# The W2 product of a fused four-layer graph kernel: one level of Strassen against two

## The chip, the cores and the metric

The kernel runs on one core of one Trainium2 chip, in fp32. The metric is the device time in microseconds of one execution. The profile gives a span, from the first to the last instruction.

## The reference

The input x is 128 graphs of 128 nodes with 256 features; adj is one 128 x 128 matrix for all graphs. Four layers follow each other, each adding its result to x:

```python
h = relu(layernorm(x)); x = x + gated_message_passing(h, adj)           # layer 0
h = relu(layernorm(x)); x = x + causal_attention(h, adj, Wqkv, Wo)      # layer 1
h = relu(layernorm(x)); x = x + gcn(h, adj * adj, W1, W2, W3)           # layer 2
h = relu(layernorm(x)); x = x + gcn_batchnorm(h, adj, bW1, bW2, ...)    # layer 3
# gcn:  h = relu(A @ (h @ W1));  h = relu(A @ (h @ W2));  return A @ (h @ W3)
```

W1 is 256 x 512, W2 is 512 x 1024, W3 is 1024 x 256. The change concerns `h @ W2`, which for each node is the largest product of the whole chain. A batch normalisation in layer 3 needs the mean and variance over all nodes, so layer 3 ends only when all graphs have passed.

## The kernel before, in words

The 128 graphs go in 32 groups of four (`G = 4`, `NG = 32`), T = 512 nodes a group. In the first pass every group runs through layers 0 to 2 and the first half of layer 3 in SBUF; its x goes to DRAM as `X3` (POOL's queue), its layer-3 values as `Z` (SP's queue). The second pass reads `Z` and `X3` again and finishes layer 3.

*Strassen.* Most weight products use the Winograd form of Strassen's algorithm at one level: seven products of quarter matrices for eight. `seven_of` makes the weights' sums once, `sums` makes the sums of an activation on DVE (four element-wise operations), and `seven` runs the products in the order 0, 1, 4, 5, 2, 6, 3 on three PSUM banks px, py, pz: products 0, 5, 6 and 3 accumulate in px, 4 and 2 in pz. Between them partial results leave the bank: `kept` copies px or pz to SBUF on ACT, and `put` adds such a copy to a bank on DVE (three of the four outputs) or copies it on ACT (the fourth). So a product that accumulates on px has to wait for the engine that reads px before it.

*The W2 product.* `layer1` ends with u = relu(.. @ W1) and uT = (A u) transposed: 32 matmuls `pmu`, four evictions of 128 x 512 by DVE in `mixed`, and `sums` over uT. `layer2` then computes h2T = relu(W2^T uT) in two halves, `wide(0)` and `wide(1)`, each a `seven` with products of four matmuls (two 128-row blocks of the output, two 128-deep pieces, 256 columns moving: `columns_by_half`, L404). `put` adds on DVE (L678) and ACT applies ReLU (L679); after the last product come the four sums of that half (L370 to L373). Then the product with W3 (`rows_by_half`, L387: 128 columns moving), `pr` with a2T, the addition to x and the store to `X3`. W2 and its sums lie in SBUF for the whole pass.

*The order.* The layers are generators; each `yield` ends a step. One turn of the group loop runs layer 2 of group g, layer 1 of g+1, layer 0 of g+2 and layer 3 of g-1, and the string `TURN` says which generator does its next step: A layer 0, B layer 1, C layer 2, D layer 3, b and d the first steps of the next ones. The last group has the string `FINAL`, and `FILL` starts the first groups. What the string gives is the program order on all engines; the framework then orders each engine's instructions by when they are ready, with program order as priority, and places the waits. PSUM is eight banks, all of one pool.

```python
    TURN = "CCCBCCABBDABBCABBDDCBADCDDBDCCDBACBCCABCCACbBCBBCBCBBCBCBCdB"
    ...
    for g in range(NG):
        if g + AHEAD < NG:
            load_x(g + AHEAD)
        ...
        for k in TURN if g < LAST else FINAL:
            next(stream[k], None)
```

Of the kernel before, what the change touches and what calls it, by code (L numbers as in the profile page):

```python
# [8 lines left out]
FP = mybir.dt.float32  # L9
AF = mybir.ActivationFunctionType  # L10
ALU = mybir.AluOpType
# [11 lines left out]
def kernel(  # L23
# [60 lines left out]
    def rows(w):  # L84
        return w.rearrange("(c p) f -> p c f", p=P)
# [29 lines left out]
    w1 = weights.tile([P, DC, H1], FP, name="w1")  # L115
    w2 = weights.tile([P, HC1, H2], FP, name="w2")
    w3 = weights.tile([P, HC2, D], FP, name="w3")
# [54 lines left out]
    dinv = small.tile([P, 1], FP, name="dinv", bufs=1)  # L172

    nc.sync.dma_start(wqkv, rows(Wqkv))
    nc.sync.dma_start(wo, rows(Wo))
# [62 lines left out]
    for dst, src in ((ain, adj_sb), (aout, adjT)):  # L238
        nc.vector.tensor_scalar(pos, src, 0.0, None, ALU.is_gt)
        nc.vector.scalar_tensor_tensor(f, src, 0.0, pos, ALU.min, ALU.add)  # L240
        nc.vector.tensor_tensor(dst, f, adj_sb, ALU.mult)

    SETS = {}
    plain = {"qv": 0, "u": 0}

    def prepare():
# [22 lines left out]
        yield  # L269
        SETS["2"] = seven_of(w2, "w2")  # L270
        yield
# [92 lines left out]
    def sums(engine, a, extra, s3=None):  # L364


        a11, a12, a21, a22 = a
        s3 = a21 if s3 is None else s3
        s1, s2, s4 = (extra[:, i] for i in range(3))
        engine.tensor_tensor(s1, a21, a22, ALU.add)  # L370
        engine.tensor_tensor(s2, s1, a11, ALU.subtract)
        engine.tensor_tensor(s4, a12, s2, ALU.subtract)
        engine.tensor_tensor(s3, a11, a21, ALU.subtract)  # L373
        return a11, a12, s4, a22, s1, s2, s3

    def quarters_t(aT):

        return quarters(aT)
# [33 lines left out]
    def seven(product, put, shape, name, pool=None):  # L412

        def kept(pb, i):
            t = (pool or w).tile(shape, FP, tag="kept", name=f"{name}_t{i}", bufs=6)
            nc.scalar.copy(t, pb)  # L419
            return t  # L420

        px = bank(shape, f"{name}_x")
        product(0, px, True)
        t1 = kept(px, 1)
        yield
        py = bank(shape, f"{name}_y")
        product(1, py, True)
        put((0, 0), py, t1)
        yield
        pz = bank(shape, f"{name}_z")  # L430
        product(4, pz, True)
        t5 = kept(pz, 5)
        yield
        product(5, px, False)
        t2 = kept(px, 2)
        yield
        product(2, pz, False)
        put((0, 1), pz, t2)
        yield
        product(6, px, False)  # L440
        put((1, 1), px, t5)
        yield
        product(3, px, False)
        put((1, 0), px, None)
        yield

    def layer0(g, bs=ALL):
# [42 lines left out]
        mine = slice(bs[0], bs[-1] + 1)  # L490
        nc.vector.tensor_copy(cmbT[:, mine, :], pc)
        yield
# [13 lines left out]
    def layer1(g, bs=ALL):  # L506
# [93 lines left out]
        pT = tile_of(g, bs, [P, G, P], "pT", f"pT_{g}", 1)[:, bs[0] : bs[-1] + 1, :]  # L600
        nc.vector.tensor_copy(pT, pp)
        yield
# [35 lines left out]
        else:  # L638
# [9 lines left out]
            yield  # L648
        uT = tile_of(g, bs, [P, HC1, T], "uT", f"uT_{g}", 1)
        mixed(uT, u, a2T, f"pmu_{tail}", (nc.vector.tensor_copy,), bs)  # L650
        if bs[-1] == G - 1:
            ex = w.tile([P, 3, HC1 // 2, T // 2], FP, tag="us", name=f"us_{g}", bufs=1)
            US[g] = sums(nc.vector, quarters_t(uT), ex)
        yield

    def layer2(g):

        xt, us = X[g], US[g]
        h2T = w.tile([P, HC2, T], FP, tag="h2T", name=f"h2T_{g}", bufs=1)

        a11, a12, a21, a22 = quarters_t(h2T)
        ex = w.tile([P, 3, HC2 // 2, T // 2], FP, tag="h2s", name=f"h2s_{g}", bufs=1)
        h2s = (a11, a12, ex[:, 2], a22, ex[:, 0], ex[:, 1], a21)

        def wide(q):
            def put(ij, pb, other):
                i, j = ij
                j = j * HC2 // 2 + 2 * q
                dst = h2T[:, j : j + 2, i * T // 2 : (i + 1) * T // 2]
                if other is None:  # L670
                    nc.scalar.activation(dst, pb, AF.Relu)
                    mine = slice(2 * q, 2 * q + 2)
                    sums(
                        nc.vector,
                        [a[:, mine] for a in (a11, a12, a21, a22)], ex[:, :, mine],
                    )
                else:
                    nc.vector.tensor_tensor(dst, pb, other, ALU.add)  # L678
                    nc.scalar.activation(dst, dst, AF.Relu)  # L679

            return seven(
                columns_by_half(us, SETS["2"], 2 * q), put, [P, 2, T // 2], f"p2_{g}_{q}"
            )

# [11 lines left out]

        yield from wide(0)
        late = wide(1)
        for _ in range(6):
            yield next(late)  # L700
# [13 lines left out]
    def layer3(g):  # L714
# [3 lines left out]
        gT = w.tile([P, DC, T], FP, tag="dT", name=f"gT_{g}", bufs=2)  # L718
        mixed(gT, h, ahT, f"pg_{g}", (nc.vector.tensor_copy,))
        ex = w.tile([P, 3, 1, T // 2], FP, tag="ex", name=f"gs_{g}", bufs=2)  # L720
# [30 lines left out]

    TURN = "CCCBCCABBDABBCABBDDCBADCDDBDCCDBACBCCABCCACbBCBBCBCBBCBCBCdB"

# [5 lines left out]
    def part(f, g):  # L759
        return f(g) if 0 <= g < NG else iter(())  # L760
# [14 lines left out]
    assert all(next(stream[k], k) == k for k in "acbdA")  # L775
    bs, ds = part(layer1, 1), stream["p"]
    next(bs)
    for g in range(NG):
# [217 lines left out]
```

## Time and profile before

| | |
|---|---|
| time before, median of 2 runs | 2605.85 us (2605.66 to 2606.03) |
| the profiled execution | 2605.08 us, span 2603.0 us |
| one turn in the middle of the first pass | 70.80 us |
| first pass, prologue included | to about 2322 us |
| second pass and output | to 2603 us |

The profile names an instruction by its line in the kernel, its engine and operation, and the tiles it writes and reads; "128x512 f32" is partitions by elements. PE is the matmul engine and PEld its weight loads, which overlap; DVE, ACT and POOL are the vector, scalar and general engines; SPq is the queue of SyncE, from which most transfers are issued. Each fp32 matmul of the source is two records. "Idle before <- releaser" says how long an engine stood and which instruction ended the wait.

### The profile page before, as it was taken

To read this page: it belongs to the slowest core of one execution; us is meant where nothing else is said; L and a number is where in the kernel's file an instruction comes from. 1 tells how busy PE (TensorE), PEld (TensorE's weight loads), DVE (VectorE), ACT (ScalarE), POOL (GpSimd) and SP (SyncE) were. 2 spreads that over 40 slices of the span, in tenths; PEclk is the share of its full clock that TensorE was granted. 3 is DMA by queue.
4 is the path that set the end of the run, shared out by engine and by line. 5 is a ranking of instruction groups with operands and counts; after the bars stand their busy time and mean duration, and the time that the engine had idled before them with its cause. 6 is when DMAs were issued, how large, how long until landed. Compare 5 with 4: busy or idle time off the path is not lost.

```text
span 2603.0 us, 40680 instructions
## 1 busy us (share of the span) xinstructions
PE 2538.9 (98%) x15281; PEld 2283.6 (88%) x15281; DVE 1914.1 (74%) x4820; ACT 1283.8 (49%) x2575; POOL 291.3 (11%) x581
## 2 busy tenths in 40 slices
PE   5999999999999999999999999999999999999996
PEld 4899999999999999999999999999999999888875
DVE  7777777777777777777777777777777776567776
ACT  4544454444445444454444444554445444346656
POOL 2110111111110111111111110111011111000001
PEclk8999999999999999999999999999999999999998
DMA  3000000000100000000000000010000000035449
GB/s 133 15 33 33 33 28 22 33 33 34 33 25 25 33 33 33 33 33 21 29 33 33 33 25 25 33 33 33 33 33 25 25 25 25 25 136 181 175 172 395
DMA packets 49560, 143.06 MB, mean 55 GB/s; under 512 B 4162, under 2 KB 23124, under 8 KB 45396
## 3 DMA queue, kind: packets, MB, share of 16 engines
q1 hardware_dynamic: 42164, 116.48, 12.3%
q0 software_dynamic: 6480, 23.60, 2.5%
q8 instruction: 120, 1.97, 0.3%
q14 instruction: 76, 0.62, 0.1%
q10 hardware_dynamic: 720, 0.39, 0.1%
HBM read 73.48 MB, written 66.98 MB: 54 GB/s over the span
## 4 chain that ended last, share of the span: by engine, by line
PE 91%; ACT 3%; DVE 2%; DMA 2%; issue 1%; POOL 1%; DVEq 0%; SPq 0%; ACTq 0%; POOLq 0%
PE p_x L404 17%; PE p_x L387 9%; PE p_z L404 8%; PE pmu L359 4%; PE p_z L387 4%; PE pz_x L404 4%; PE p_y L404 4%; PE pu_x L387 4%; PE po_x L879 3%; PE pg L359 2%; PE ps L577 2%; PE pm L359 2%; PE pm L497 2%; PE p_y L387 2%; PE pqv_x L534 2%; PE pr L707 2%
## 5 line engine op out<-in xcount | busy, mean ns | idle before, releaser
L345 ACT ACTIVATE h<-x,sh,rs 128x256 f32<-128x256 f32 x512 | 268.9, 590 | 370.5 <-POOL sh L342 370.5
L404 PE MATMUL p_x<-uT,w 128*128 128x256 f32 x1024 | 242.2, 379 | 0.0
L679 ACT ACTIVATE h2T<-h2T 128x512 f32<-128x512 f32 x192 | 120.5, 628 | 229.0 <-DVE h2T L678 228.5
L404 PEld LDWEIGHTS p_x<-uT,w 128*128 128x128 f32 x1024 | 189.7, 190 | 23.2
L334 DVE BATCH_NORM_STATS2 st<-x 128x6 f32<-128x256 f32 x512 | 191.4, 416 | 3.9 <-DMA x<-in_x_dram 1.8
L338 POOL TENSOR_SCALAR rs<-mv 128x4 f32<-128x4 f32 (+1 forms) x131 | 31.1, 237 | 1393.8 <-ACT h2T L679 1026.9
L456 DVE SCALAR_TENSOR_TENSOR gs<-h,gw 128x256 f32<-128x256 f32 x384 | 161.9, 422 | 33.4 <-ACT h L345 27.5
L419 ACT COPY p_t<-p_x 128x512 f32<-128x512 f32 (+1 forms) x192 | 96.8, 504 | 108.4 <-PE p_x L404 101.6
L339 POOL TENSOR_TENSOR rs<-rs,nhalf 128x4 f32<-128x4 f32 (+1 forms) x131 | 149.5, 1141 | 0.0
L359 PEld LDWEIGHTS pmu<-a2T,u 128*128 128x128 f32 x1024 | 119.4, 192 | 15.3 <-issue 15.1
L387 PEld LDWEIGHTS p_x<-w,h2T 128*128 128x128 f32 x1024 | 124.3, 192 | 3.3
L387 PE MATMUL p_x<-w,h2T 128*128 128x128 f32 x1024 | 124.6, 275 | 0.0
L632 ACT ACTIVATE u<-u 128x512 f32<-128x512 f32 x93 | 58.7, 631 | 133.7 <-DVE u L631 133.7
L868 ACT ACTIVATE zi<-zi,sh_bn,sc_bn 128x512 f32<-128x512 f32 x124 | 97.3, 812 | 49.1 <-DMA zi<-z 19.8
L404 PE MATMUL p_x<-us,w_s 128*128 128x256 f32 x512 | 121.3, 379 | 0.0
L404 PE MATMUL p_z<-us,w 128*128 128x256 f32 x512 | 121.2, 379 | 0.0
L404 PE MATMUL p_x<-uT,w_s 128*128 128x256 f32 x512 | 121.1, 379 | 0.0
L404 PE MATMUL p_y<-uT,w 128*128 128x256 f32 x512 | 121.0, 379 | 0.0
L404 PE MATMUL p_z<-us,w_s 128*128 128x256 f32 x512 | 120.9, 379 | 0.0
L359 PE MATMUL pmu<-a2T,u 128*128 128x128 f32 x1024 | 119.5, 275 | 0.0
L708 DVE TENSOR_TENSOR x<-pr,x 128x512 f32<-128x512 f32 x64 | 43.7, 683 | 90.4 <-PE pr L707 90.4
L404 PEld LDWEIGHTS p_z<-us,w 128*128 128x128 f32 x512 | 97.2, 190 | 13.6 <-ACT p_t L419 0.4
(300 smaller groups left out, 6183.8 us busy)
## 6 DMA issues: line engine op xcount, KB each, us to landing
z<-zo SPq DMA_DIRECT2D x62, 512.0 KB, 2.6
zi<-z SPq DMA_DIRECT2D x31, 1024.0 KB, 4.8
x<-x POOLq DMA_DIRECT2D x32, 512.0 KB, 3.4
x<-in_x_dram SPq DMA_DIRECT2D x31, 512.0 KB, 4.0
out_dram<-x3i SPq DMA_DIRECT2D x30, 512.0 KB, 12.3
x3i<-x SPq DMA_DIRECT2D x19, 512.0 KB, 5.1
x3i<-x POOLq DMA_DIRECT2D x13, 512.0 KB, 11.5
w<-in_L_gnn_W_dram SPq DMA_DIRECT2D x1, 2048.0 KB
```

The costliest lines, as they stand in the source:

```text
L334: nc.vector.bn_stats(st[:, k, :], xt[:, b, :])
L339: nc.gpsimd.tensor_tensor(rs, rs, nhalf[:, :n], ALU.pow)
L345: nc.scalar.activation(h[:, b, :], xt[:, b, :], AF.Relu, bias=sh[:, k : k + 1], scale=rs[:, k : k + 1])
L359: nc.tensor.matmul(pm[:, k, :], src[:, b, c * P : (c + 1) * P], aT, start=True, stop=True)
L387: nc.tensor.matmul(pb[:, rr, :], a_r[r][:, c, rr * P : (rr + 1) * P], b_r[r][:, c, :wide], start=(first and rr == 0 and c == 0), stop=(c = ...
L404: nc.tensor.matmul(pb[:, jj, :], b_r[r][:, c, at : at + P], a_r[r][:, c, :], start=(first and jj == 0 and c == 0), stop=(c == nk - 1), ski ...
L419: nc.scalar.copy(t, pb)
L456: nc.vector.scalar_tensor_tensor(gs, h[:, b, :], 1.0, gw[:, i, :], ALU.mult, ALU.mult, accum_out=gl[:, k, i : i + 1],)
L632: nc.scalar.activation(dst, dst, AF.Relu)
L679: nc.scalar.activation(dst, dst, AF.Relu)
L868: nc.scalar.activation(z, z, AF.Relu, bias=sh1[:, j : j + 1], scale=sc1[:, j : j + 1],)
L879: nc.tensor.matmul(pb, BW2R[r][:, c, :], a_r[r][:, c, :], start=(first and c == 0), stop=(c == FC // 2 - 1), skip_group_check=True,)
```

## The change

W2's product goes from one level of Strassen to two: each of the seven products of quarters is itself done by seven products of sixteenths, 49 in all, each of two matmuls with 128 columns moving and no accumulation over depth. In detail:

- `prepare_w2` replaces `seven_of(w2)`: it makes the seven weights of the first level and, of each, the seven of the second, on DVE, and stores them in DRAM as `W2R`. W2 no longer has its own place in SBUF; during preparation it lies in the buffer that later holds uT.
- `load_w2` reads one of the seven sets (128 x 7 x 256 floats) for each part of each group, on SP's queue, into three rotating buffers.
- The end of `layer1` writes uT in a new layout with room for all second-level sums; its evictions alternate between DVE and ACT; the sums are eleven operations.
- `layer2` runs seven parts in the order 0, 1, 4, 5, 2, 6, 3. Each is one `seven` with 128 x 256 results that go to one of seven homes; additions on whole quarters (128 x 1024) then form h2T's quarters, ReLU on ACT works on whole quarters, and `sums` runs once over the whole h2T.
- Copies that move from DVE to ACT: `cmbT` in layer 0, `pT` in layer 1, one of two gT evictions in layer 3. `kept` has five buffers for six.
- `TURN` is another string with the same steps.

```diff
-    w2 = weights.tile([P, HC1, H2], FP, name="w2")
...
+    def load_w2(r, n):
+        SETS["2", r] = weights.tile([P, 7, H2 // 4], FP, tag="w2r", name=f"w2_{n}_{r}", bufs=3)
+        nc.sync.dma_start(SETS["2", r], W2R[r])
+
+    def prepare_w2():
+        b11, b21, b12, b22 = quarters(w2)
+        t1, t2, t4n = w2t
+        nc.vector.tensor_tensor(t1, b12, b11, ALU.subtract)
+        nc.vector.tensor_tensor(t2, b22, t1, ALU.subtract)
+        nc.vector.tensor_tensor(t4n, b21, t2, ALU.subtract)
+        nc.vector.tensor_tensor(b12, b22, b12, ALU.subtract)
+        stage = None
+        for n, r in enumerate(SEVEN):
+            b = (b11, b21, b22, t4n, t1, t2, b12)[r]
...
+            nc.vector.tensor_tensor(ex[:, 0], c12, c11, ALU.subtract)
+            nc.vector.tensor_tensor(ex[:, 1], c22, ex[:, 0], ALU.subtract)
+            nc.vector.tensor_tensor(ex[:, 2], c21, ex[:, 1], ALU.subtract)
+            nc.vector.tensor_tensor(c12, c22, c12, ALU.subtract)
+            nc.sync.dma_start(
+                W2R[r][:, :4, :].rearrange("p (c h) f -> p c h f", c=2),
+                b.rearrange("p c (h f) -> p c h f", h=2),
+            )
+            nc.sync.dma_start(W2R[r][:, 4:, :], ex)
+
+    SEVEN = 0, 1, 4, 5, 2, 6, 3
...
-        SETS["2"] = seven_of(w2, "w2")
+        prepare_w2()
...
-            t = (pool or w).tile(shape, FP, tag="kept", name=f"{name}_t{i}", bufs=6)
+            t = (pool or w).tile(shape, FP, tag="kept", name=f"{name}_t{i}", bufs=5)
...
-        nc.vector.tensor_copy(cmbT[:, mine, :], pc)
+        nc.scalar.copy(cmbT[:, mine, :], pc)
...
-        nc.vector.tensor_copy(pT, pp)
+        nc.scalar.copy(pT, pp)
...
-        uT = tile_of(g, bs, [P, HC1, T], "uT", f"uT_{g}", 1)
-        mixed(uT, u, a2T, f"pmu_{tail}", (nc.vector.tensor_copy,), bs)
...
+            evict = nc.scalar.copy if c % 2 else nc.vector.tensor_copy
+            evict(dst, pm.rearrange("p (i b) n -> p i (b n)", b=2))
...
+            three(0, 2)
+            s1, s2, s4, s3 = v[:, 4], v[:, 5], v[:, 2], v[:, 6]
+            nc.vector.tensor_tensor(s1, v[:, 6], v[:, 3], ALU.add)
+            nc.vector.tensor_tensor(s2, s1, v[:, 0], ALU.subtract)
+            nc.vector.tensor_tensor(s4, v[:, 1], s2, ALU.subtract)
+            nc.vector.tensor_tensor(s3, v[:, 0], v[:, 6], ALU.subtract)
+            three(2, 7)
+            fourth(0, 7)
...
+            def product(s, pb, first):
+                for jj in range(2):
+                    nc.tensor.matmul(
+                        pb[:, jj, :], b_s[s][:, jj * P : (jj + 1) * P], a_s[s],
+                        start=(first and jj == 0), stop=True, skip_group_check=True,
+                    )
...
+        def wide():
+            x_, t1, t2 = (ex[:, i] for i in range(3))
+            homes = {0: x_, 1: a11, 4: a22, 5: t1, 2: a12, 6: t2, 3: a21}
+            then = {
+                0: (), 1: ((a11, x_),), 4: (), 5: ((x_, t1),), 2: ((a12, a22), (a12, x_)),
+                6: ((x_, t2), (a22, x_)), 3: ((a21, x_),),
+            }
+            for n, r in enumerate(SEVEN):
+                if n < 6:
+                    load_w2(SEVEN[n + 1], g)
+                elif g < LAST:
+                    load_w2(SEVEN[0], g + 1)
+                of_r = one_of_seven(r, homes[r])
+                for _ in range(3):
+                    next(of_r)
+                yield
+                for _ in of_r:
+                    pass
+                for dst, src in then[r]:
+                    add(dst, src)
+                if then[r] and r != 5:
+                    relu(then[r][-1][0])
+                yield
+            sums(nc.vector, (a11, a12, a21, a22), ex)
...
-        mixed(gT, h, ahT, f"pg_{g}", (nc.vector.tensor_copy,))
+        mixed(gT, h, ahT, f"pg_{g}", (nc.scalar.copy, nc.vector.tensor_copy))
...
-    TURN = "CCCBCCABBDABBCABBDDCBADCDDBDCCDBACBCCABCCACbBCBBCBCBBCBCBCdB"
+    TURN = "CBCACDCABCBBBDDBBACCCABCDBDCDACBDBBCCACCBCBBBABDbBCCBCCBCCBd"
```

`three(lo, hi)` makes three of the four second-level sums for the parts lo to hi - 1 at once; `fourth(0, 7)` makes the last one for all seven parts, in place. In the text, w0a and w0b are the two steps of the part r = 0: the products 0, 1, 4, and then 5, 2, 6, 3.

## The prediction

> **What bounds the kernel now.** I read the page's busy times and slices first, then the windows of one turn, then the timelines of PE and DVE inside that turn, and last the waits of the DMA queue. The page:
>
> ```profile
> PE 2538.9 (98%) x15281; PEld 2283.6 (88%) x15281; DVE 1914.1 (74%) x4820; ACT 1283.8 (49%) x2575; POOL 291.3 (11%) x581
> ...
> PE   5999999999999999999999999999999999999996
> ...
> DVE  7777777777777777777777777777777776567776
> ```
>
> PE is full from the second slice on; DVE runs at seven tenths. In the windows of one turn (us; then busy us and instructions of PE, PEld, DVE, ACT, POOL; granted clock; DMA share; GB/s), whole, and cut where the second half of the W2 product has its sums:
>
> ```profile
> 1062.40:1133.20 70.80, 70.80 (x440) 64.53 (x439) 52.84 (x138) 34.33 (x70) 8.66 (x18) 1.00 0.08 31
> 1062.40:1113.00 50.60, 50.60 (x297) 46.11 (x296) 43.56 (x115) 26.63 (x56) 6.84 (x14) 1.00 0.10 37
> 1113.00:1133.20 20.20, 20.20 (x145) 18.42 (x144) 9.28 (x24) 7.69 (x15) 1.81 (x4) 1.00 0.04 15
> ```
>
> A turn is 70.8 us with no idle PE time at all. DVE has 18.0 us to spare, but unevenly: 7.0 us in the first 50.6 us (86% busy) and 10.9 us in the tail. The PE timeline gives the two matmul rates:
>
> ```profile
> 1062.41 1.89 PE L404 MATMUL p_x<-uT,w 128*128 128x256 f32 x8
> 1064.14 1.89 PE L404 MATMUL p_y<-uT,w 128*128 128x256 f32 x8
> ...
> 1109.35 1.95 PE L387 MATMUL p_y<-w,h2T 128*128 128x128 f32 x16
> 1111.13 1.95 PE L359 MATMUL pm<-a2T,h 128*128 128x128 f32 x16
> ```
>
> Each matmul of the source is two records. Start to start, four of 256 columns take 1.73 us (0.4325 each), eight of 128 columns 1.78 us (0.223 each): half the columns cost 52%, weight loads included. For DVE, start to start:
>
> ```profile
> 21.94 1.21 DVE L214 TENSOR_TENSOR w_s<-w 128x1024 f32<-128x1024 f32 x1
> 23.07 0.61 DVE L476 SCALAR_TENSOR_TENSOR m<-aout,gt,m 128x128 f32<-128x128 f32 x2
> ...
> 1079.13 0.42 DVE L373 TENSOR_TENSOR gT<-gT 128x256 f32<-128x256 f32 x1
> 1079.46 0.43 DVE L372 TENSOR_TENSOR gs<-gT,gs 128x256 f32<-128x256 f32 x1
> ...
> 1111.51 0.68 DVE L373 TENSOR_TENSOR h2T<-h2T 128x512 f32<-128x512 f32 x1
> 1112.11 0.68 DVE L372 TENSOR_TENSOR h2s<-h2T,h2s 128x512 f32<-128x512 f32 x1
> ```
>
> So packed DVE work costs 0.335 us for 256 elements, 0.60 for 512, 1.13 for 1024; between these I interpolate (640: 0.73; 896: 1.0).
>
> **What the Trainium skill says.** "VectorE: DVE Perf Modes", the perf-mode tier table: fp32 tensor_tensor has only the single rate, and with any PSUM operand too. The trace agrees: 0.69 us for 512 elements in L372 (SBUF) and in L678 (PSUM), so every added sum is paid by the element. "Perfetto Trace Analysis", Matmuls: independent groups should rotate through PSUM banks so that an eviction overlaps the next group, and larger matmuls are more efficient. The trace agrees on both: 0.223 is more than half of 0.4325, and no product waits for its eviction here, because each is followed by 0.9 to 1.8 us of other products.
>
> **The change, part by part.**
>
> *PE.* Removed per group: 14 products of four 256-column matmuls, 14 x 1.73 = 24.2 us. Added: 98 of 128 columns, 98 x 0.223 = 21.9 us. Gain 2.3 us a turn, all on the path; a turn of pure PE would be 68.5 us.
>
> *DVE, removed per turn:* 6 additions and 8 sums of layer2 at 512, 4 sums of uT, 2 of 4 uT evictions, and the copies cmbT, pT and one gT that go to ACT: 23 x 0.60 = 13.8 us. *Added:* sums of uT: three of 256, four of 512, three of 640, one of 896 (1.0 + 2.4 + 2.2 + 1.0 = 6.6 us); 21 PSUM additions of 256 (7.0); seven additions of 1024 that join the quarters (7.9); four sums of 1024 (4.5). Together 26.0, net +12.2. DVE has 52.8 + 12.2 = 65.0 us of work in a 68.5 us turn, 95%: its spare time falls from 18.0 to 3.5 us. This is the heart of the case.
>
> *ACT.* Five more copies of 512 (0.5 us packed), 28 copies of 256 (0.3) for 6 copies and 2 ReLUs of 512, four ReLUs of 1024 for six of 512: about 14.7 added, 7.2 removed. 34.3 becomes 42 us, 61%: no bound, but it now stands between products that follow each other closely.
>
> *The new waits.* (1) One product is now 0.45 us of PE, and inside the second half of each of the 49-product's seven parts the order is 5, 2, 6, 3: product 3 writes the bank that DVE must have read after product 6, with nothing between in the source. A 256-element DVE read is 0.42 us, behind whatever DVE has in hand. Other PE work must be moved in. That the order does this is seen in the first turn of before, where a product is split so that pp and pc get in as they become ready:
>
> ```profile
> 105.26 0.59 PE L404 MATMUL p_x<-us,w_s 128*128 128x256 f32 x2
> 105.69 0.38 PE L599 MATMUL pp<-ident,p 128*128 128x128 f32 x2
> ```
>
> There is no idle PE time around it, so I count most of these waits as filled. (2) The last uT eviction is followed by 6.6 us of sums, and the very last (`fourth`) makes the operand of product 6 of the first part. It is ready about 0.75 + 6.6 = 7.4 us after the last pmu matmul; PE reaches product 6 after w0a (1.34), hT (0.87) and two products (0.9), 3.1 us. That is a hole of 4.3 us each turn; before, the whole uT sums were 2.4 us and first needed after two products of 1.73. The second part's products, gT and its like can fill it. Bounds: 0 if all is filled, 4.3 if nothing is; I take 2.2. (3) DVE starts each turn 6.6 us behind, and by the running sum of the steps in the new turn (from its start to the end of the part r=6: PE 37.2 us, DVE 37.0) it catches up only in the tail. PE then meets DVE at nearly every part; for DVE and ACT arriving late I take 0.8 us a turn, bounds 0 and 4. The cover that hid such waits, DVE's 18 us, is gone. Total stall taken: 3.0 us, turn 68.5 + 3.0 = 71.5.
>
> *DMA.* Seven loads of 128 x 7168 B (0.92 MB) a turn. The page has 4.0 us from issue to landing for 512 KB and 4.8 for 1 MB, so about 4.7; three buffers let a load start when the product three before it is done, some 6 us of its own PE work ahead. 6.4 MB over 71 us adds 90 GB/s to 31; the second pass moves 170 to 180 at under half DMA share. Free, if the loads are not held in SP's queue:
>
> ```profile
> SPq L108 <- DMA x<-x: 1062.0, 28, 60.9
> ```
>
> The load of x stands in SP about 38 us a turn waiting for the X3 store of the group before; W2 loads queued behind it would come late. SP's issues are ordered by readiness (in the prologue the load for group 3 is at 25.6 us, ahead of BW2T's store at 81.8, which the source has first), and the three buffers are filled by then, so I take 0; the other end is 5 us a turn.
>
> *Ends.* prepare_w2 is 4 x 1.13 + 28 x 0.335 = 13.9 us of DVE against 4.5, in a prologue where PE is busy 116 of 145 us: +6 taken (0 to 10). The last turn has no other group's work to fill: its PE gain is lost again in the 4.5 us of late sums before the third product and in hole (2), which gives +4 (0 to 10).
>
> **Sum.** Against the profiled execution (2605.08, span 2603.0, so 2.1 us lie around it): 31 turns x (71.5 - 70.8) = +22, ends +10: 2637; the median shown is 0.8 higher: 2638 us. A difference under 2% (52 us) can't be told from no change in this kernel.
>
> **The rivals.**
> - *Clean fill* (chance 0.12): stall under 1 us, say 0.5. For it: PE shows not one gap in a steady turn of before. Against: 95% DVE. 31 x (69.0 - 70.8) + 8 = -48: 2558, and 2541 with no stall.
> - *DVE becomes the bound* (0.36): slower. In a turn of before DVE is idle in a dozen places for data (3.5 for p_z, 2.8 for pr, 1.7 for ACT's mT). If 9 of the 18 us of such idling cannot be packed, the turn is 65.0 + 9 = 74 us: 31 x 3.2 + 10 = +109: 2715. It decides from 70.8 - 65.0 = 5.8 us of DVE idle time a turn; every us above costs 31. For it: the pmu evictions, pr and the two sums that follow each other leave the tail thin in DVE work (8 us of idling there by the running sum) while the front has none to spare. Against: the new turn puts the parts 5 us apart.
> - *W2 loads late* (0.07): 5 us of PE waiting a turn on DMA and part of the gain kept: 31 x 3.5 + 10: 2725.
> - *No gain on PE*: 128-column matmuls bound by weight loads. The L387 rate already contains them (16 loads in 1.78 us); 0.02, about 2700 with the stalls.
> - *Forecast, gain eaten* (0.43): stall 1.5 to 4.5 us, 2591 to 2685, likeliest 2638.
>
> **How the numbers follow.** Clean fill gives 0.07 of "faster" and 0.05 of "same"; the forecast 0.38 "same", 0.05 "slower"; DVE bound 0.32 "slower", 0.04 "same"; the rest is slower. Faster 0.07, same 0.47, slower 0.46. The range leaves out the best of the clean fills and the worst of the DVE-bound cases: 2560 to 2750.
>
> **What would show it.** Right: PE busy near 96% of a steady turn of 71 to 72 us, DVE at 63 to 66 us of it, PE's waits naming DVE sums of uT at product 6 and DVE additions at product 3, no wait on w2. Wrong: DVE work far from 65 us, PE waits on the W2 loads, a turn under 70, or PE idle on ACT copies, which I hold hidden.

## The result, and the profile after

The changed kernel takes 2834.41 us (median of two runs, 2832.83 to 2835.99) against 2605.85: 1.0877 times as long (95% interval 1.083 to 1.0924), slower by 229 us. The forecast was 2638, the range 2560 to 2750; the time lies outside it. The profiled execution took 2835.99 us with a span of 2834.2.

The page of after, busy times:

```profile
PE 2624.6 (93%) x17969; PEld 2374.0 (84%) x17969; DVE 2279.3 (80%) x5484; ACT 1510.8 (53%) x3315; POOL 355.3 (13%) x581
```

PE is no longer full: 98% became 93%, and at a lower granted clock (0.968 over the execution, 0.992 before), so a part of its "busy" time is slow time. DVE went from 74% to 80%. Two turns of after, in the windows (us; then busy us and instructions of PE, PEld, DVE, ACT, POOL; granted clock; DMA share; GB/s):

```profile
1009.64:1088.39 78.75, 74.42 (x523) 68.11 (x522) 63.87 (x158) 41.43 (x93) 10.90 (x17) 0.96 0.32 109
1323.95:1399.47 75.52, 71.36 (x524) 65.60 (x523) 63.85 (x158) 41.43 (x93) 10.23 (x17) 1.00 0.34 114
```

Same work, but 78.75 us at clock 0.96 and 75.52 us at clock 1.00. Before, every steady turn was 70.79 or 70.80 us; now the 29 turns between the first and the last range from 75.5 to 80.1 us, 77.87 on average. That is the first thing to see: one part of the loss is always there, another comes and goes.

The part that is always there is a hole, a stretch in which PE stands, that begins 6.8 us into a turn. The turn that starts at 1009.64, from the timeline:

```profile
1013.21 0.61 PE L748 MATMUL p_x<-uT,w 128*128 128x128 f32 x4
...
1014.18 0.41 DVE L407 TENSOR_TENSOR uT<-uT 128x256 f32<-128x256 f32 x1
...
1015.09 2.63 POOL L379 TENSOR_TENSOR sh<-sh,rs 128x4 f32<-128x4 f32 x1
...
1016.07 0.39 PE L748 MATMUL p_x<-uT,w 128*128 128x128 f32 x2
...
1016.98 0.69 DVE L722 TENSOR_TENSOR uT<-uT 128x512 f32<-128x512 f32 x1
1017.76 2.07 ACT L382 ACTIVATE h<-x,sh,rs 128x256 f32<-128x256 f32 x4 [3.76 <-POOL sh L379]
1019.74 0.35 ACT L457 COPY p_t<-p_x 128x256 f32<-128x256 f32 x1
...
1020.14 1.22 PE L748 MATMUL p_x<-uT,w 128*128 128x128 f32 x4 [3.69 <-ACT p_t L457]
1021.16 1.06 PE L748 MATMUL p_z<-uT,w 128*128 128x128 f32 x4
```

Read it backwards from the 3.69 us in which PE stood. Product 5 of the part r = 0 adds to px, so it waits until ACT has copied product 0 out of px (L457). That copy takes 0.35 us and px was complete by 1013.8, but on ACT it stands behind `h` of layer 3's norm (L382, four activations, 2.07 us), and `h` waits for GpSimd's `sh` (L379), the multiplication of two 128 x 4 tiles. That operation took 2.63 us here; it ends with the run of VectorE's uT sums that began ahead of it. The wait of 3.69 us comes in each of the 29 turns between the first and the last, and is the largest of PE's (us in total, times, longest):

```profile
PE p_x L748 <- ACT p_t L457: 109.4, 31, 3.7
```

The same chain in before, in the turn that starts at 1058.84 (L342 is the shift, L345 `h`, L419 the copy, and the product at 1068.47 is product 5):

```profile
1062.98 0.20 POOL L342 TENSOR_TENSOR sh<-sh,rs 128x4 f32<-128x4 f32 x1
1063.22 2.08 ACT L345 ACTIVATE h<-x,sh,rs 128x256 f32<-128x256 f32 x4 [5.29 <-POOL sh L342]
...
1065.20 0.56 ACT L419 COPY p_t<-p_x 128x512 f32<-128x512 f32 x1
...
1068.47 1.89 PE L404 MATMUL p_x<-us,w_s 128*128 128x256 f32 x8
```

The copy stood behind `h` in before too. But there the norm's step was ahead of the sums in the string, the shift took 0.20 us, and the copy was done 6.9 us into the turn (1065.76), while PE came to product 5 after 9.6 us: 2.7 us to spare. In after the copy is done 10.45 us into the turn (1020.09), 3.5 later, of which the drawn-out shift is 2.4, and PE would come to product 5 after 6.65 us (1016.29), 3.0 earlier, because the products ahead of it are short. 2.7 - 3.5 - 3.0 is a lateness of 3.8 us. The new order and the short products make about half of it each.

The part that comes and goes is the clock. In the turn at 1009.64, the records of a product behind the hole (p_z above) take 1.06 us, and one product follows the other after 0.85 us. The turn at 1323.95 has the same hole, and its products behind it are at full rate, 0.61 us and every 0.45:

```profile
1334.44 0.71 PE L748 MATMUL p_x<-uT,w 128*128 128x128 f32 x4 [3.69 <-ACT p_t L457]
...
1336.11 0.61 PE L748 MATMUL p_z<-uT,w 128*128 128x128 f32 x4
```

The granted clock was one half for 6.82 us of the first turn, from within the hole on:

```profile
1018.70:1025.52 6.82, 5.38 (x25) 5.38 (x26) 5.40 (x10) 3.26 (x9) 0.00 (x0) 0.50 0.23 79
```

The Trainium skill, "TensorE: Matmul & The Clock Gate", Part 1, says that an idle window of about 3.4 us halves TensorE's clock until it has been busy for about as long again, and that the window runs freely, so that the moment varies. The trace agrees that it varies, and on the length: with the same 3.69 us of waiting, 12 of the 29 turns have a stretch of 3.41 us at half rate, 12 have one of 6.83, and five have none. Those five take 76.06 us on average (one 75.52, four 76.2), so the half rate is worth 77.87 - 76.06 = 1.8 us a turn. The trace does not agree on 3.4 us of idling as a lower limit: PE had stood for 2.0 to 3.1 us in the 3.41 us before each of the 24 stretches, and in runs below, waits of 2.97, 2.84 and 2.09 us were followed by half rate in some turns.

W2's loads answered the forecast, from the page's DMA issues (KB each, us to landing):

```profile
w<-W2R SPq DMA_DIRECT2D x224, 896.0 KB, 4.7
```

No product of a steady turn waits for one. The last turn has the only long one, 2.93 us.

Where the 231.2 us between the two spans went: from the first pmu matmul of the first turn to that of the last group are 31 turns, 2401.8 us after and 2187.8 before, +214.0; the prologue is +8.2 (81.3 against 73.1 us), what follows the last turn +9.0.

### The profile page after: what moved, and what is told of

It reads as the page before. It is cut to its first block, busy times and chain, and to the rows that moved or that the text cites. A ratio compares the mean times of both kernels' runs of the same rounds, so it can differ in the third digit from the quotient of the medians.

```text
span 2834.2 us, 48744 instructions
## 1 busy us (share of the span) xinstructions
PE 2624.6 (93%) x17969; PEld 2374.0 (84%) x17969; DVE 2279.3 (80%) x5484; ACT 1510.8 (53%) x3315; POOL 355.3 (13%) x581
## 5 line engine op out<-in xcount | busy, mean ns | idle before, releaser
L748 PE MATMUL p_x<-uT,w 128*128 128x128 f32 x3584 | 557.4, 282 | 116.2 <-ACT p_t L457 109.4
L748 PEld LDWEIGHTS p_x<-uT,w 128*128 128x128 f32 x3584 | 495.5, 194 | 146.7 <-ACT p_t L457 121.7
L382 ACT ACTIVATE h<-x,sh,rs 128x256 f32<-128x256 f32 x512 | 266.2, 589 | 300.6 <-POOL sh L379 300.6
L457 ACT COPY p_t<-p_x 128x256 f32<-128x256 f32 x512 | 189.8, 371 | 276.6 <-PE p_x L748 160.5
L748 PE MATMUL p_z<-uT,w 128*128 128x128 f32 x1792 | 303.4, 292 | 13.3 <-DVE uT L407 11.3
L748 PEld LDWEIGHTS p_z<-uT,w 128*128 128x128 f32 x1792 | 260.7, 204 | 28.4 <-DVE uT L407 17.2
L764 DVE TENSOR_TENSOR h2T<-h2T,h2s 128x1024 f32<-128x1024 f32 x128 | 155.7, 1216 | 48.0 <-ACT h2T L757 48.0
L767 ACT ACTIVATE h2T<-h2T 128x1024 f32<-128x1024 f32 x128 | 135.4, 1058 | 62.6 <-DVE h2T L764 62.5
L457 ACT COPY p_t<-p_z 128x256 f32<-128x256 f32 x256 | 93.8, 366 | 130.5 <-PE p_z L425 73.2
L748 PE MATMUL p_y<-uT,w 128*128 128x128 f32 x896 | 157.4, 290 | 0.0
L748 PEld LDWEIGHTS p_y<-uT,w 128*128 128x128 f32 x896 | 133.0, 206 | 0.0
L379 POOL TENSOR_TENSOR sh<-sh,rs 128x4 f32<-128x4 f32 (+1 forms) x131 | 123.5, 943 | 10.1
```

What stands on the lines that cost most here:

```text
L379: nc.gpsimd.tensor_tensor(sh, sh, rs, ALU.mult)
L382: nc.scalar.activation(h[:, b, :], xt[:, b, :], AF.Relu, bias=sh[:, k : k + 1], scale=rs[:, k : k + 1])
L748: nc.tensor.matmul(pb[:, jj, :], b_s[s][:, jj * P : (jj + 1) * P], a_s[s], start=(first and jj == 0), stop=True, skip_group_check=True,)
L764: nc.vector.tensor_tensor(dst, dst, src, ALU.add)
```

## The experiments

Reading a turn: "excess" below is the time from start to start of PE's matmuls less the same matmuls at full rate (0.223 us for 128 columns, 0.4325 for 256), summed over one turn where it is more than 0.1 us. Before has none; after has 6.6 in the turn at 1323.95 and 7.2 on average over the five turns at full clock. All ratios are to the kernel before, run beside each on the same chip.

**One level against two, old order against new.** Three runs complete a table. The first keeps before's product and order and only moves the evictions (cmbT, pT, one gT, every second uT) to ACT; the second adds the new string; the third is after with the old string.

```diff
-    TURN = "CCCBCCABBDABBCABBDDCBADCDDBDCCDBACBCCABCCACbBCBBCBCBBCBCBCdB"   # before
+    TURN = "CBCACDCABCBBBDDBBACCCABCDBDCDACBDBBCCACCBCBBBABDbBCCBCCBCCBd"   # after
```

> One part alone on the kernel before: the copies cmbT, pT, one gT of two and every second uT go from DVE to ACT; W2's product stays at one level, the turn string is the old one. Theory: the second ACT eviction of uT stands behind the norm's h, so the uT sums come late for the third product and PE waits: up to 2 us a turn, 2610 to 2670. Rival, moving copies to ACT is free since ACT is half idle: within 0.3% of 2606.

> Before with the moved evictions and the new order of the turn, the product with W2 still at one level (14 products of 1.73 us): the change without its second level. It differs from the run with the moved evictions alone (2651.8 us) only in the order. Theory B1 (the order at the turn's start is harmful by itself): the hole of some 4 us and the half clock after it are there too, 2720 to 2800 us. Theory B2 (it needs the short products): 1.73 us products cover the late copy, 2630 to 2690 us.

> Changed: only the turn string, which is that of the kernel before. Theory: the old string has the norm ahead of uT (hole of e1's kind remains through the ACT eviction of uT) and three C steps running at its start, so the sums are needed sooner and DVE has less time: 2800 to 2950. Rival, the new string itself is what costs: faster than 2780.

| | old order | new order |
|---|---|---|
| one level, evictions moved | 2651.8 us, 1.0173 [1.0157, 1.0188] | 2765.1 us, 1.0602 [1.0586, 1.0618] |
| two levels | 2973.2 us, 1.1402 [1.1385, 1.1419] | 2834.4 us, 1.0877 [1.083, 1.0924] |

The moved evictions alone cost 45 us beside before on the same chip (2606.8); the new order costs 113 us where the products are long and saves 139 where they are short. The second level costs 321 us in the old order, 69 in the new. (Old order with two levels came out above the 2800 to 2950 that was expected; its turns have a wait of 2.84 us for the uT sums and one of 2.98 later.) So the new order is fitted to the short products, and the loss isn't its fault alone. The run with one level and the new order has the same chain at the start of the turn, behind long products. Its timeline (the norm is L345, the copy L419, and the products of 256 columns L404):

```profile
1062.34 1.89 PE L404 MATMUL p_x<-uT,w 128*128 128x256 f32 x8
...
1064.22 1.96 POOL L342 TENSOR_TENSOR sh<-sh,rs 128x4 f32<-128x4 f32 x1
...
1066.21 2.08 ACT L345 ACTIVATE h<-x,sh,rs 128x256 f32<-128x256 f32 x4 [3.08 <-POOL sh L342]
...
1068.19 0.57 ACT L419 COPY p_t<-p_x 128x512 f32<-128x512 f32 x1
1068.40 1.95 PE L359 MATMUL pg<-ahT,h 128*128 128x128 f32 x16
1070.19 0.38 PE L404 MATMUL p_x<-us,w_s 128*128 128x256 f32 x1
```

The shift is drawn out (1.96 us), `h` takes 2.08, the copy comes behind it; PE does not stand at all. From the end of product 0 to its next use of px it has 6.1 us of other work (pt, p_y, p_z and pg, from 1064.07 to 1070.19); in after it had about 2.0 (p_y, p_z, pt and one matmul pair). What the run's turn of 76.06 us has over before's 70.79 comes mostly from four other waits of 0.73 to 1.34 us (three on ACT copies, one on a DVE addition), at clock 1.00. So its time is in the range of B1 (the order harms by itself), and its start is that of B2 (the hole needs short products): the new order does harm long products, but not there.

**Is it the amount of VectorE's work?** This was the likeliest of the prediction's rivals. One run takes work away from after: the seven 1024-element additions that join the outer products are left out.

```diff
-                for dst, src in then[r]:
-                    add(dst, src)
```

> After, without the seven VectorE additions of 1024 elements that join the seven products of the outer level (7 x 1.22 us = 8.5 us of VectorE a turn; the parts are left unjoined, so the output differs). VectorE's busy time falls from 63.9 to about 55.4 us a turn, near that of before (52.8), and ScalarE and TensorE keep what they do. Theory A (VectorE's amount of work leaves no slack, so every release comes late): turn 70 to 72 us, 2570 to 2640 us. Theory B (the chain at the turn's start, GpSimd's shift drawn out beside the sums, then h, then the copy, with the half clock after it): the start keeps its 4 to 7 us, only the small holes later close: turn 75 to 77 us, 2720 to 2780 us.

2905.5 us, 1.1139 [1.112, 1.1157], slower than after. Its window:

```profile
1042.21:1121.84 79.63, 73.21 (x523) 67.02 (x522) 57.00 (x151) 41.50 (x93) 10.97 (x17) 0.98 0.31 108
```

DVE fell to 57.0 us (72% of the turn), and the start kept its 3.69 us wait on the copy, with half rate after it in each of the 29 steady turns (none is under 79.6 us). Neither theory foresaw a loss. The framework also ordered the rest otherwise (a wait of 1.29 us on an ACT copy behind pm that after doesn't have, and smaller ones of 0.3 and 0.4), and why that came out slower is not settled. So less work on VectorE did not shorten the start's hole; but since the order changed with it, the run does not clear the amount of work altogether. The opposite run adds 24 VectorE additions of 256 elements a group to before:

```diff
                     nc.scalar.activation(dst, dst, AF.Relu)
+                for _ in range(3):
+                    nc.vector.tensor_tensor(dump, w3[:, 0, :], w3[:, 2, :], ALU.add)
```

> Before, plus 24 VectorE additions of two SBUF tiles of 256 elements a turn (three after each put of the product with W2, results thrown away): about 24 x 0.42 = 10 us, which takes VectorE from 52.8 to about 63 us a turn, as in after, while products stay 1.73 us long. Theory A (VectorE's amount of work): turn 74 us or more, 2700 us or more. Theory B (short products and the turn's order, not the amount): the 1.73 us products cover the later releases, turn 70.8 to 72.5 us, 2606 to 2660 us.

2662.3 us, 1.0209 [1.0194, 1.0224], just above the range of theory B and well below that of theory A. The additions depend on nothing, and the framework put all 768 into the first half of the turns, which makes two experiments of one:

```profile
600.08:673.14 73.06, 71.91 (x440) 64.34 (x439) 70.21 (x190) 33.51 (x70) 8.04 (x17) 1.00 0.09 30
1329.80:1400.59 70.79, 70.79 (x439) 64.52 (x438) 52.81 (x138) 34.47 (x70) 8.66 (x17) 1.00 0.08 30
```

With 17.4 us more on VectorE, 96% busy, this turn takes 73.06 us; without, 70.79. Over the first fourteen turns the additions cost 54 us, 3.9 a turn (from 2.3 to 7.3 in the steady ones). So a VectorE more loaded than after's (63.9 us) costs before 3.9 us a turn on average; after loses 7.1, with a PE that has 2.3 us less to do. The amount of work costs something, then, but in before it does not make the whole loss; what it costs behind short products is not shown.

**The loads of W2.** All loads but the first three are left out; later parts use those three in turn.

```diff
-        SETS["2", r] = weights.tile(...)
-        nc.sync.dma_start(SETS["2", r], W2R[r])
+        k = SEVEN.index(r) % 3
+        if k not in HELD:
+            HELD[k] = weights.tile(...)
+            nc.sync.dma_start(HELD[k], W2R[r])
+        SETS["2", r] = HELD[k]
```

> Left out: all W2 loads but the first three sets, which all groups and parts then use; the products are the same in number and shape, their values are not those of the reference. Theory: the loads cost nothing in a steady turn, within 1% of 2834, and only the wait of 2.9 us in the last turn goes. Rival, the 0.92 MB loads slow the turn by their traffic or by SP's queue: faster by 2% or more.

2832.9 us, 1.0866 [1.085, 1.0882], as after. The loads cost nothing that shows.

**Mending the chain at the start.** The norm's step is put ahead of the sums again:

```diff
-    TURN = "...BCCBCCBCCBd"
+    TURN = "...BCCBCCBCCdB"
```

> Changed: the last two letters of the turn string, so that the norm of layer 3 comes ahead of the uT step in program order, as in the kernel before. No work is added or removed. Theory (ACT stands in order behind the norm's h, which waits for POOL's last multiply, which runs 2.63 us beside DVE's uT sums): POOL is done before the sums, the 3.7 us hole and the slow clock after it (some 2.7 us) go, the turn falls from 78.75 to about 72.5 us, the time to about 2640. Rival, the uT sums are late by themselves (operand of product 6): the hole stays at 3 to 4 us with another engine named, time within 1% of 2834. Rival, DVE is the bound: the same, since DVE's work is unchanged.

2794.8 us, 1.0713 [1.0696, 1.0731]. A miss by 150 us: the shift is short again, and the hole has moved.

```profile
1074.34 0.20 POOL L379 TENSOR_TENSOR sh<-sh,rs 128x4 f32<-128x4 f32 x1
1074.58 2.07 ACT L382 ACTIVATE h<-x,sh,rs 128x256 f32<-128x256 f32 x4 [1.81 <-POOL sh L379]
...
1076.56 0.56 ACT L704 COPY uT<-pmu 128x512 f32<-128x512 f32 x1
...
1077.15 0.46 DVE L407 TENSOR_TENSOR uT<-uT 128x256 f32<-128x256 f32 x1 [1.79 <-ACT uT L704]
...
1077.66 0.71 PE L748 MATMUL p_z<-uT,w 128*128 128x128 f32 x4 [2.84 <-DVE uT L407]
```

Now a uT eviction stands behind `h` on ACT, the sums wait for it, and PE waits 2.84 us for the sums, at half rate after it in this turn.

The shift of layer 3's norm as one VectorE operation:

```diff
-        nc.gpsimd.tensor_scalar(sh, mv[:, :, 0], -1.0, None, ALU.mult)
-        nc.gpsimd.tensor_tensor(sh, sh, rs, ALU.mult)
+        if layer == 3:
+            nc.vector.scalar_tensor_tensor(sh, mv[:, :, 0], -1.0, rs, ALU.mult, ALU.mult)
+        else: ...                        # as before
```

> Changed: in the norm of layer 3 alone, POOL's two operations for the shift are one DVE operation on 4 elements (about 0.16 us); the turn string is that of the changed kernel. Theory: POOL's stretched multiply leaves the chain, h starts 1 to 3 us earlier, the hole shrinks to under 2 us and the clock stays up: about 2650 to 2740, according to where DVE's order puts the new operation among the sums. Rivals (late sums, DVE as the bound): within 1% of 2834, DVE having even a little more to do.

2753.2 us, 1.056 [1.0545, 1.0576]: 75.0 us a turn, at clock 1.00 in all steady turns but one, and 81 us less than after. The hole shrank as expected, to 1.79 us; the time is 13 us above the range that was expected. VectorE pays: the shift stands at the head of its queue until GpSimd's power is done, and the sums come late.

```profile
1058.04 0.16 DVE L379 SCALAR_TENSOR_TENSOR sh<-mv,rs 128x4 f32<-128x4 f32 x1 [1.24 <-POOL rs L376]
...
1059.25 0.71 PE L751 MATMUL p_z<-uT,w 128*128 128x128 f32 x4 [1.79 <-DVE uT L410]
```

The first string change with all uT evictions on VectorE, and then that with the shift of every norm on VectorE:

```diff
-            evict = nc.scalar.copy if c % 2 else nc.vector.tensor_copy      # uT
+            evict = nc.vector.tensor_copy
```

> Changed: e1_norm_before_sums, and all four uT evictions are on DVE again, as in the kernel before (DVE +1.2 us a turn). In e1 the second ACT eviction of uT stood behind the norm's h (1076.56, sums from 1077.15) and PE waited 2.8 us for the sums. Theory (ACT's queue order, not the amount of work on any engine, makes the hole): the sums start about 2.5 us earlier, the turn falls from 76.7 to 72 to 74 us, time about 2650 to 2710. Rival, DVE as the bound: DVE's work grows, so the time is that of e1 or up to 1% more.

> Changed: e5_swap_and_vector_evicts, and in all norms the two POOL operations for the shift are one DVE operation (four a turn, about 0.4 us packed). Theory: POOL's multiply that is stretched beside DVE sums (1.18 us in the norm of layer 0) leaves the chain; if ACT's h is on PE's path there, up to 1.5 us a turn less than e5, about 2620 to 2690. Rival, DVE as the bound: 0.4 us a turn more than e5 (+0.5%).

2787.6 us (1.0693 [1.0677, 1.0709]) and 2830.2 (1.0852 [1.0834, 1.087]), both misses. The start's hole is down to 0.77 us in the first, but two waits on ACT copies of 1.47 and 1.36 us open at pz; in the second one of these is 2.09 us, and in some turns the clock halves there.

Layer 3's norm one step into the next turn, so that the copy stands ahead of `h`; then that with the shift on VectorE:

```diff
-    TURN = "CBCACDC...BCCBCCBCCBd"
+    TURN = "CBCDACDC...BCCBCCBCCB"     # FINAL gets one D more
```

> After, with layer 3's norm in the next turn's fourth step instead of the last step of this one (d is taken from the end of the string, D is put in after CBC, FINAL gets one D more). On VectorE and GpSimd the order at the turn's start stays; on ScalarE the copy p_t of product 0 now stands ahead of h, and the copy of p_z behind h's first part, which still waits for GpSimd's shift. Theory B (the order of ScalarE's queue beside the late shift makes the hole): product 5 no longer waits, the hole of 3.85 us becomes 1 to 3 us at product 2 or later, turn 76 to 78 us, 2750 to 2815 us. Rival (the chain is as long whatever stands first): hole 3.5 us or more, 2825 to 2860 us.

> The same with layer 3's shift as one VectorE operation: h no longer waits for GpSimd's stretched multiplication, but VectorE stands about 1.2 us at the shift for the power on GpSimd. Theory B: less than the 75.0 us a turn of the shift alone, 73 to 75 us, 2690 to 2755 us. Rival (what is mended at the start is lost elsewhere): 2755 to 2830 us.

2807.1 us (1.0765 [1.0724, 1.0806]) and 2748.6 (1.0554 [1.0537, 1.0572]), both in the ranges of the theory of ACT's queue, and both near their upper ends. In the first the hole is at product 2 now, behind the copy of p_z, and a little shorter, as that theory had it. The second can't be told from the shift on VectorE alone (1.056), so there the later norm adds nothing that shows. The first also shows the clock once more, in the windows of two turns:

```profile
1070.91:1149.32 78.41, 74.81 (x524) 68.50 (x523) 63.75 (x158) 41.31 (x93) 10.89 (x17) 0.96 0.33 110
1765.03:1839.81 74.78, 71.33 (x524) 65.59 (x523) 63.75 (x158) 41.32 (x93) 10.21 (x17) 1.00 0.34 115
```

Each has one hole of this kind (waits of 2.98 and 2.97 us), and in the first the products behind it follow each other every 0.85 us. The two turns differ by 3.6 us, of which two small waits at other places (0.2 and 0.3 us of excess) make a part.

**Evictions back.** After, with every moved eviction on VectorE again:

```diff
-        nc.scalar.copy(cmbT[:, mine, :], pc)                  # pT, one gT, every second uT alike
+        nc.vector.tensor_copy(cmbT[:, mine, :], pc)
```

> After, with all the evictions that the change moved to ScalarE (cmbT, pT, one gT, every second uT) back on VectorE: VectorE +3.4 us a turn (63.9 to 67.3), ScalarE -3.4. Theory B: the copy p_t still stands behind h in ScalarE's queue and VectorE is later still: 2820 to 2900 us. Rival (the moved evictions crowd ScalarE and open the holes): 2700 to 2780 us.

2899.9 us, 1.1122 [1.1106, 1.1139]: the moves suit the two-level product; they are not its trouble. The time is at the upper end of theory B's range, but its hole is another one: PE waits 3.00 us for `h` itself (L382, at pg), not for the copy p_t.

**Keeping TensorE awake.** 32 transposes of the identity are put into the hole of each turn:

```diff
                     next(of_r)
                 yield
+                if n == 0 and 0 < g < LAST - 1:
+                    awake(32)
```

> Changed: 32 transposes of the identity (3.5 us of PE, result unused) are put into the place of the hole at the start of each turn, so that PE doesn't stand idle there. Nothing is removed. If the matmuls at half rate after the hole come from the idle time itself: granted clock near 0.99, about 2.7 us a turn back less what the transposes overhang, 2750 to 2790. If they are slow for another reason (operands, PSUM): no gain, 2834 or up to 3.5 us a turn more, 2940.

2881.8 us, 1.1052 [1.1035, 1.1068], 79.2 to 79.5 us a turn, in the range of the rival that saw no gain. The products right behind the transposes are at full rate, but then PE waits 2.01 us for `fourth` (L715), and in some turns half rate follows there and pg is slow; the clock's share can't be read from this run.

**Distance between dependent products.** First the seven inner products in two stages: the last four (5, 2, 6, 3) of one outer product interleaved with the first three of the next; then that with the shift on VectorE.

```diff
-                for _ in range(3):
-                    next(of_r)
-                yield
-                for _ in of_r:
-                    pass
+                for i in range(3):
+                    next(of_r)
+                    if of_q:
+                        next(of_q)               # the outer product before
+                    if i == 1:
+                        yield
+                if of_q:
+                    ends(of_q, q)                # its rest, joins and ReLU
+                of_q, q = of_r, r
```

> After, with the seven inner products of one outer product run in two stages: its last four (5, 2, 6, 3) are interleaved with the first three (0, 1, 4) of the next outer product, so that other products stand between two that need the same bank. Instructions, amounts and the turn's string are unchanged. Theory C (short products too close to each other: what a late copy costs is its lateness less the work between dependent products): the holes of 0.5 us and more inside the product with W2 shrink, turn 73 to 76 us, 2650 to 2760 us. Rival D (single late releases at fixed places: h behind GpSimd's shift, sums, pm): 2810 to 2860 us, as after.

> The staggered kernel with the shift of layer 3's norm as one VectorE operation, as in the run that brought after to 2753. Theory C with both: turn 71 to 73 us, 2600 to 2670 us. Rival D: about the 2753 of the shift alone, 2730 to 2780 us.

2970.2 us (1.139 [1.1371, 1.1409]) and 2913.4 (1.1174 [1.1158, 1.1191]): both missed the range of theory C, by 200 us and more, and that of the rival too. In every second turn of the first the start still waits 3.88 us, and p_z of the product with W3 waits 2.77 us for the h2 sums; in the turns between, the start waits 2.7 us for the uT sums. W2's loads show in every steady turn, mostly with 0.3 to 0.7 us and once with 3.1. The stagger tests more than it was meant to.

Then products twice as long in after itself: each pair of matmuls is issued twice.

```diff
-                for jj in range(2):
+                for n in range(4):
+                    jj = n % 2
...
-                        start=(first and jj == 0), stop=True, skip_group_check=True,
+                        start=(first and n == 0), stop=True, skip_group_check=True,
```

> After, with each of the 98 pairs of matmuls of the product with W2 issued twice (the output is therefore not the reference's): TensorE gets 98 x 0.223 = 21.9 us more a turn, 68.5 to 90.4 us without a hole, and VectorE and ScalarE keep all they do. Theory C (a late release costs its lateness less the TensorE work that lies between dependent products): the holes and the half clock close nearly, turn 91 to 93.5 us. Rival D (single late releases at fixed places stop TensorE whatever lies between): the excess of 10.3 us stays at 7 us or more, turn 97.5 to 101 us.

3541.0 us, 1.3587 [1.3564, 1.3609], 99.7 or 101 us a turn: a miss for theory C, the theory of distance, as it was put, and in the range of its rival. The first matmuls of the turn that starts at 1075.08:

```profile
1078.65 1.06 PE L749 MATMUL p_x<-uT,w 128*128 128x128 f32 x8
...
1085.57 2.08 PE L749 MATMUL p_x<-uT,w 128*128 128x128 f32 x8 [3.21 <-ACT p_t L457]
```

Product 5 starts 10.49 us after the turn's start; in after it was 1020.14 - 1009.64 = 10.50. The release has its own pace (uT's evictions and sums, shift, `h`, copy), and PE's added work didn't move it. The framework put 2.7 us of other work (p_y, p_z, pt) between the two uses of px here, not the 6.1 that it put there in the one-level run, so the hole stayed, 3.21 us for 3.69. Together the two runs fit this reading: what counts is not the length of a product by itself, but the work that the fixed order holds between a product and its bank's next use, against a release that comes late.

## Why the prediction was wrong

*What was right.* PE's gain: a turn at full rate without holes was put at 68.5 us; after's is 75.52 - 6.64 = 68.9. VectorE: 65.0 forecast, 63.9 measured. ACT: 42, measured 41.4. W2's loads: free, 4.7 us landing. New wait (1), product 3 after 6: filled, as assumed; no wait of that kind is above 0.5 us in the turns shown. The direction was left open: slower had a chance of 0.46, no change 0.47.

*The step that failed* is the stall term, 3.0 us a turn; it was 77.87 - 68.9 = 9.0. By its parts:
- The hole at the turn's start: nothing in the sum for it; measured are 3.85 us at product 5 and 0.53 ahead of it at p_z, 4.4 together. ACT was costed at nothing ("no bound, but it now stands between products"), and its copies held hidden. I summed ACT's work and did not look at what stands ahead of a copy in its queue. That no product of before waits for its eviction was read rightly; that product 5 had only 2.7 us to spare there, and that the short products alone would take 3.0, was not worked out.
- GpSimd had no line at all: the norm's step, moved from ahead of the sums to behind them, met them there. The Trainium skill has this in "GPSIMD Engine Reference", Specifications: GpSimd's SBUF interfaces are shared with VectorE, with contention where a VectorE instruction has two SBUF inputs. The trace agrees: 0.20 us in the run with the norm ahead of the sums, 2.63 beside them. A step that is moved has to be costed with what it lands beside.
- Wait (2), the hole at product 6 for `fourth`: 2.2 taken, and in after's turns it is filled. It came up only where transposes were put in. Of the uT sums, only the first is late for PE, at p_z.
- Wait (3), VectorE and ACT late elsewhere: 0.8 taken; 2.8 measured (7.2 of excess at full clock less 4.4 at the start), 1.1 of them at pm, where PE takes `h` as fast as ACT makes it.
- The half clock after a hole, 1.8 us on average, was not in the sum, nor in any rival.

Over the turns the forecast was 31 x 0.7 = 22 us; measured 214. The ends were put at +10 and are 17.2, of which the prologue 8.2 (taken 6) and the end 9.0 (taken 4). That no difference under 52 us could be told was too cautious: the 45 us of the moved evictions came out as 1.0157 to 1.0188.

*The rival "VectorE becomes the bound"* came nearer in time (2715), but VectorE is busy for 63.9 of 77.87 us, and PE's longest wait is for an ACT copy behind GpSimd. Taking 7 us from VectorE didn't help, though the order changed with it, and adding 17 to before cost 3.9 us a turn. What the traces point to is the order in which each engine takes its work, fixed beforehand, with waits of 2 to 3 us at the head of a queue and 2 us of other work on PE to cover them.

*What stays open.* The rearrangements of after moved its holes; none closed them all. The best, 2748.6 us, gets back 86 of the 229 us and still has 5.3 to 5.9 us of excess in a turn (1.95 at p_z for the sums, 0.6 to 1.3 at pz, 1.1 at pm). Whether some order would bring the two-level product to its 68.9 us was not shown, and no run beat before. Nor is it settled why leaving out the joins made the kernel slower, or how much of the loss elsewhere goes with the amount of VectorE's work.

## What to carry to other kernels

Before making TensorE's pieces shorter, list for every bank that is used again what the engine that empties it has ahead of that copy in its queue, and compare the worst of these waits with the PE work that lies between; a sum of busy times can't show it. When a step is moved, cost it beside its new neighbours on every engine, GpSimd's small operations too. And price a hole of some 3 us on TensorE with the slow matmuls that may follow it.

## What the runs showed of the hardware

- A GpSimd multiplication of two 128 x 4 tiles took 0.20 us alone and 1.96 to 2.63 us beside back-to-back VectorE additions of two SBUF tiles; it ended with their run.
- At half rate a product of the W2 part took 0.85 us instead of 0.45. The half rate came in stretches of 3.41 or 6.83 us, in 24 of after's 29 turns between the first and the last, and PE had stood for 2.0 to 3.1 of the 3.41 us before each. The same 3.69 us wait was followed by one in some turns and not in others: 75.5 to 80.1 us a turn. Waits of 2.84 and 2.97 us, and one of 2.09 in another run, were followed by half rate in some turns too; in the turn shown with a longest wait of 1.79 us the granted clock was 1.00, but one other turn of that run had a stretch at half rate with 1.4 us of standing ahead of it.
